# First cross attention of a decoder: queries and keys projected once, the partners of the rotation moved by a shuffle on VectorE

## The chip, the core and the metric

The kernel runs on one core of a Trainium2 chip. The metric is the device time of one launch in microseconds (us). A core has five engines that are named here as the profile names them: PE (TensorE, matrix products; PEld are its weight loads), DVE (VectorE), ACT (ScalarE), POOL (GpSimd) and SP (SyncE, which issues transfers). Each engine works through its own list of instructions in the order of the program, and the engines wait for each other by semaphores.

## What is computed

The reference is a decoder of two layers on 16 sequences of 128 x 256 numbers. The first layer is a causal self-attention with ternary weights, a cross attention with rotary positions, and a mixture of experts; the second has a self-attention, a plain cross attention and a last feed-forward part. A layer norm follows each. The change concerns the first cross attention alone:

```python
q = jnp.einsum('oi,bit->bot', wq, x) + bq[None, :, None]
k = jnp.einsum('oi,bit->bot', wk, c) + bk[None, :, None]
v = jnp.einsum('oi,bit->bot', wv, c) + bv[None, :, None]
...
x_rope, x_pass = (x[..., :d], x[..., d:])
d2 = d // 2
neg_half = jnp.concatenate([-x_rope[..., d2:], x_rope[..., :d2]], axis=-1)
x_rope = x_rope * cos + neg_half * sin
return jnp.concatenate([x_rope, x_pass], axis=-1)
```

There are 16 heads of 8 channels. Of each head, the first four channels are rotated (d = 4): channel 0 is paired with channel 2, and channel 1 with channel 3. In the kernel channels are the 128 partitions, so the partner of a row is the row two below it or two above it.

## The kernel before, in words

The weights are loaded first and the weights of the first attention are made ternary. Then the first self-attention and the first cross attention of all 16 batches are written out as one schedule of beats (`by_beats`, L274). The self-attention (`ternary`, L686) gives two beats to a batch, and the cross attention (`rope_cross_plain`, L906) gives eight, so the beats of the cross attention begin at number 32. A beat holds up to two groups of head scores, then the sums over values, then jobs. Each job has an offset from the first beat of its batch; a job of batch b with offset o is put in beat 32 + 8b + o. Jobs of one beat are issued in the order of their list.

Every instruction of PE, and all those issued through `vec`, `act` and `pool`, keep the order in which they are written (`Written`, L190, and `mm`, L238). So an instruction of an engine that has to wait holds up all that come behind it on that engine.

In a beat of the cross attention (`cross_scores`, L428), PE makes two score tiles named `ps_st`. One has queries in its partitions; DVE takes its row maxima (`nm`). The other has keys in its partitions, is 11 beats behind, and has the maxima added to it by a small product with a 0/1 table (`nmT`, `pick`); ACT takes its exponential into `pT`. Two beats later, PE multiplies these by the values into `ps_o`.

The jobs of a batch in the cross attention are these, with their offsets: `keys` (-10) and `queries` (-5) project and rotate; `values` (5) projects the values; `parts` (8) splits the maxima into three bf16 parts on DVE, and `maxima` (9) transposes them on PE; `out` (20) copies the sums with ACT, `spread` (21) shuffles the denominators on DVE, `invert` (22) takes a logarithm and an exponential of them on ACT, and `divide` (25) multiplies on DVE; `finish` (26) is the output projection with the residual and the statistics of the norm, `scale_rows` (27) applies the norm to the rows of x. For the experts that follow, `gate_turn` (28), and for each pair of batches `gate` (32), `gate_best` (33), `gate_rows` (35) and `places` (39), choose experts and places; four scatters from POOL follow.

Accumulators lie in PSUM. From beat 45 on (`switch`, L265), there are three buffers for score tiles, one for `ps_o`, and one single buffer named `ps_m` for all the products of jobs (L267 and L268): a job's product can only be written once the product before it has been read.

A projection with its rotation (`side`, L920) is now made of two products. One has the weights as they are, and one has the rows of the weights in the order of the partners. Both go into one `ps_m` tile. `rotated` (L800) then adds the bias to the first half and multiplies by the cosines in one DVE instruction, adds the bias to the second half on ACT, multiplies that by the signed sines on POOL, and adds the two on POOL. For queries, POOL then makes four copies of the result (`z`), each with the channels of one head of four left and the others zero.

Another path (`rope_cross_masked`, L984) serves masks that take pairs out. It isn't taken with the inputs here, since the mask has ones alone, but it shares `rotated` and the tables, so it is edited too.

Of the kernel before, what the change touches and what calls it, by code (L numbers as in the profile page):

```python
# [9 lines left out]
F32 = mybir.dt.float32  # L10
# [3 lines left out]
AF = mybir.ActivationFunctionType  # L14
ALU = mybir.AluOpType
# [3 lines left out]
P = 128  # L19
D = 256  # L20
# [11 lines left out]
def kernel(ctx: ExitStack, tc: tile.TileContext, a: dict, out: bass.AP):  # L32
    nc = tc.nc
# [22 lines left out]
    cpool = attn.enter_context(tc.tile_pool(name="ctxpool", bufs=1))  # L56
# [5 lines left out]
    hm = load(const, [P, 26], a["head_masks"], "hm", eng=nc.scalar)  # L62
# [89 lines left out]
    nc.gpsimd.memset(zero, 0.0)  # L152


    xw = load(cpool, [P, 8, P], a["xw"], "xw", eng=nc.gpsimd)
    xb = load(cpool, [P, 6], a["xb"], "xb", eng=nc.gpsimd)
    bv2 = load(cpool, [P, D], a["bv2"].partition_broadcast(P), "bv2", eng=nc.gpsimd)
    rope = load(cpool, [P, 2, D], a["rope"], "rope", eng=nc.gpsimd)
    ctx_t = [load(cpool, [P, D], a["ctx"][b], f"ctx_{b}", eng=nc.gpsimd) for b in range(B)]
# [46 lines left out]
    vec, act, pool = Written(nc.vector), Written(nc.scalar), Written(nc.gpsimd)  # L206
# [31 lines left out]
    def mm(*args, **kw):  # L238

        tc.keep_in_program_order(nc.tensor.matmul(*args, **kw))  # L240
# [391 lines left out]
    ps = pprep.tile([P, 4], F32, name="ps_prep")  # L632
# [9 lines left out]
    for w in range(4):  # L642
        t = pw0.tile([P, 2, D], F32, name="wround", bufs=2)
# [15 lines left out]
    bias = w0.tile([P, 2, D], F32, name="bias")  # L659
# [137 lines left out]
        return 2, 3, causal_scores(pl, kept, qk_scale), jobs, range(B)  # L797


    def rotated(pl, pab, n, dst):  # L800

        t0 = pl[dst].tile([P, D], F32, name=f"rot{n}")
        t1 = pl["w"].tile([P, D], F32, name="rot_t")
        vec.scalar_tensor_tensor(t0, pab[:, 0, :], xb[:, 2 * n : 2 * n + 1], rope[:, 0, :], ALU.add, ALU.mult)
        act.activation(t1, pab[:, 1, :], AF.Identity, bias=xb[:, 2 * n + 1 : 2 * n + 2])
        pool.tensor_tensor(t1, t1, rope[:, 1, :], ALU.mult)
        pool.tensor_tensor(t0, t0, t1, ALU.add)
        return t0
# [88 lines left out]
    def cross_output(pl, b, bias, *products):  # L897

        po = pl["m"].tile([P, D], F32, name="ps_m")
        for n, (w, oT) in enumerate(products):  # L900
            mm(po, lhsT=xw[:, w, :], rhs=oT, start=(n == 0), stop=(n == len(products) - 1))
        xn = pl["w"].tile([P, D], F32, name="xn")
        vec.scalar_tensor_tensor(xn, po, bias, x_t[b], ALU.add, ALU.add)
        return xn, statistics(xn)

    def rope_cross_plain(pl):  # L906

        kept = {}
        bias_of = {}

        def biases(b):

            if b:
                return
            pb = pl["m"].tile([P, 1], F32, name="ps_m")
            mm(pb, lhsT=xw[:, 5, :], rhs=xb[:, 5:6], start=True, stop=True)
            bias_of["ov"] = const.tile([P, 1], F32, name="bias_ov")
            vec.tensor_tensor(bias_of["ov"], pb, xb[:, 4:5], ALU.add)

        def side(b, n, src):  # L920
            pab = pl["m"].tile([P, 2, D], F32, name="ps_m")
            for i in range(2):
                mm(pab[:, i, :], lhsT=xw[:, 2 * n + i, :], rhs=src, start=True, stop=True)
            return rotated(pl, pab, n, "wq"[n])

        def queries(b):
            q = side(b, 0, x_t[b])
            z = pl["q"].tile([P, 4, D], F32, name="z")
            for i in range(4):
                pool.tensor_scalar_mul(z[:, i, :], q, hm[:, 2 + i : 3 + i])  # L930
            kept[b]["qz"] = z

        def keys(b):
            kept[b] = {}
            kept[b]["k"] = side(b, 1, ctx_t[b])

        def values(b):
            pv = pl["m"].tile([P, 2, P], F32, name="ps_m")
            for kc in range(2):
                mm(pv[:, kc, :], lhsT=ctx_t[b][:, kc * P : (kc + 1) * P], rhs=xw[:, 4, :], start=True, stop=True)  # L940
            v = kept[b]["v"] = v8[b % 2]
            for n in range(2):
                act.copy(
                    v[:, :, n::2, 8 * n : 8 * n + 8],
                    pv.rearrange("p c (g i n d) -> p (c g) i n d", g=4, i=2, n=2)[:, :, :, n, :],
                )

        def parts(b):
            maxima_parts(pl, kept[b]["nm"], nmx[b % 2], 4)

        def maxima(b):
            kept[b]["nmT"] = turned_maxima(pl, nmx[b % 2])

        def out(b):
            kept[b] = sums_out(pl, kept[b]["o"])

        def spread(b):
            kept[b] = kept[b], sums_on_values(pl, kept[b])

        def invert(b):  # L960
            inverted(kept[b][1])

        def divide(b):
            ol, l = kept[b]
            vec.tensor_tensor(l, ol, l, ALU.mult)

        def finish(b):
            oT = kept[b][1]
            kept[b] = cross_output(pl, b, bias_of["ov"], (6, oT[:, 0, :]), (7, oT[:, 1, :]))

        def scale_rows(b):
            xn, stats = kept.pop(b)
            scaled(x_t[b], xn, stats)

        jobs = [(8, parts), (9, maxima), (20, out), (21, spread), (22, invert), (25, divide), (-11, biases), (-10, keys),
                (-5, queries), (5, values), (26, finish), (27, scale_rows)]
        for beat, part in ((28, gate_turn), (32, gate), (33, gate_best), (35, gate_rows), (39, places)):
            jobs.append((beat, lambda b, part=part: part(pl, b)))

        for k in range(4):  # L980
            jobs.append((41 + 2 * k, lambda b, k=k: b % 2 and scatter(b - 1 + k // 2, k % 2)))
        return 8, 11, cross_scores(pl, 16, kept, 11), jobs, range(B)

    def rope_cross_masked(st):  # L984

        pl = attention_pools(st)
        v8p = padded(pl["v"], 16, "v8p")
        for b in range(B):
            rot = []
            for n, src in ((0, x_t[b]), (1, ctx_t[b])):  # L990
                pab = pl["m"].tile([P, 2, D], F32, name="ps_m")
                nc.tensor.matmul(pab[:, 0, :], lhsT=xw[:, 2 * n, :], rhs=src, start=True, stop=True)
                nc.tensor.matmul(pab[:, 1, :], lhsT=xw[:, 2 * n + 1, :], rhs=src, start=True, stop=True)
                rot.append(rotated(pl, pab, n, "w"))
            z = pl["w"].tile([P, 4, D], F32, name="z")
            for i in range(4):
                nc.vector.tensor_scalar_mul(z[:, i, :], rot[1], hm[:, 2 + i : 3 + i])
            pv = pl["m"].tile([P, 2, P], F32, name="ps_m")
            for kc in range(2):
                nc.tensor.matmul(  # L1000
                    pv[:, kc, :], lhsT=ctx_t[b][:, kc * P : (kc + 1) * P], rhs=xw[:, 4, :], start=True, stop=True
                )
            vn = pl["w"].tile([P, 2, P], F32, name="v")
            nc.vector.tensor_tensor(vn, pv, bv2.rearrange("p (c d) -> p c d", c=2), ALU.add)
            v = v8p[b % 2]
            nc.vector.tensor_copy(own_channels(v, 16), vn.rearrange("p c (h d) -> p c h d", h=16))
            oT = cross_heads(pl, 16, rot[0], [z[:, i, :] for i in range(4)], v, dict(masked, v=vn))
            xn, stats = cross_output(pl, b, xb[:, 4:5], (5, oT.rearrange("p c q -> p (c q)")))
            scaled(x_t[b], xn, stats)
            for part in (gate_turn, gate, gate_best, gate_rows, places):  # L1010
                part(pl, b)
            for k in range(4 if b % 2 else 0):
                scatter(b - 1 + k // 2, k % 2)

    taken_out = nc.values_load(n_out[0:1, 0:1], min_val=0, max_val=D * D)
    with tc.If(taken_out == 0) as cmp:
        with ExitStack() as st:
            pl, switch = attention_tiles(st, 4)
# [169 lines left out]
    with ExitStack() as st:  # L1188
        pl, switch = attention_tiles(st, 6)
# [422 lines left out]
def layouts(inputs):  # L1612
# [4 lines left out]
    row = np.arange(P)  # L1617
    c = row % 8

    mate = row + np.where(c < 2, 2, np.where(c < 4, -2, 0))  # L1620
    theta = np.float32(1.0) / np.float32(10000.0) ** (np.arange(0, 4, 2, dtype=np.float32) / np.float32(4))
    angle = np.arange(D, dtype=np.float32)[None, :] * theta[c % 2][:, None]
    turn = (c < 4)[:, None]
# [11 lines left out]
    for n in range(2):  # L1635
# [11 lines left out]
        "xw": np.stack([wq.T, wq[mate].T, wk.T, wk[mate].T, wv.T, wo.T] + pairs, 1),  # L1647
        "xb": np.stack([bq, bq[mate], bk, bk[mate], bo, i["L0_xattn_bv"]], 1),
# [44 lines left out]
```

## Time and profile before

| What | Value |
|---|---|
| Median of three runs | 1469.78 us (1468.67 to 1469.87) |
| The profiled execution's own time | 1472.02 us |
| Its span, from first to last instruction | 1470.3 us |
| Mean granted PE clock | 0.959 |
| Beats in which the cross attention runs with the self-attention | up to about 209 us |
| The rest of the first cross attention | 209.62 to some 535 us |
| ACT ACTIVATE pT<-ps_st, 128x1024 | 224 of 1.024 us |
| DVE TENSOR_REDUCE nm<-ps_st, 128x1024 | 1.22 us each |
| PE MATMUL ps_m<-x,xw and ps_m<-ctx,xw | 64 records each, four for a batch |
| DVE SCALAR_TENSOR_TENSOR rot<-ps_m,xb,rope | 32 of 0.483 us |
| ACT ACTIVATE rot_t<-ps_m,xb | 32 of 0.474 us |
| POOL TENSOR_TENSOR rot_t<-rot_t,rope and rot<-rot,rot_t | 32 each, 0.734 and 0.727 us |
| POOL TENSOR_SCALAR z<-rot,hm | 64 of 0.926 us |
| DVE STREAM_SHUFFLE l<-ol, 128x512 | 16 of 0.728 us |

One execution was recorded by the hardware profiler. Times in it are from the start of its span. A timeline row gives the start, the length, the engine, the line, the operation with the tile it writes and those it reads, and the number of instructions merged into the row; in brackets stand the idle time ahead of it and what ended it. Line 199 is a helper's line (`Written`) and so is line 240 (`mm`), so instructions are told apart by the names of their tiles. An f32 product is recorded as two instructions of PE. Granted clock is the share of the full PE clock that the chip allowed.

### The profile page before, as it was taken

Reading aid. Unit: us, or ns where it says so; the run is one execution under the profiler, and the core shown is the slowest. Engines: PE = TensorE matmul, PEld = TensorE weight load, DVE = VectorE, ACT = ScalarE, POOL = GpSimd, SP = SyncE. Lnnn points to the kernel's source line nnn. Section 1 sums busy time; section 2 is a strip of 40 time slices with the busy share of each in tenths; the row PEclk is TensorE's granted clock in tenths of the full one; section 3 lists DMA queues with packets and bytes.
Section 4 is the critical chain, followed back from the end, with each engine's and each line's share of the span. In section 5 each row is a group of like instructions: output and inputs, shape, how many; then the busy total and the mean of one; then the engine's idle time right before and its main releaser. Section 6 shows DMA issues by size and latency. Waiting matters only on the chain. (4 is left out here: it accounts for less than half of the span.)

```text
span 1470.3 us, 28836 instructions
## 1 busy us (share of the span) xinstructions
PE 1338.7 (91%) x11993; PEld 857.1 (58%) x11993; DVE 810.8 (55%) x2085; ACT 595.7 (41%) x1051; POOL 289.6 (20%) x402
## 2 busy tenths in 40 slices
PE   3999999999999938999999589999999989989997
PEld 2656555555555415777888456665555544446666
DVE  6899876777777530100110168876767656543222
ACT  1454426555655611111112135543555556761110
POOL 7000243344444120000000233312121100000000
PEclk9999989999999968999999769999999998999999
DMA  9200000000000006222330411000000000000000
GB/s 300 68 2 2 2 1 2 2 16 16 16 12 12 23 28 193 96 94 92 112 129 15 158 37 31 23 2 1 2 1 2 2 2 1 0 2 15 15 8 22
DMA packets 42780, 57.15 MB, mean 39 GB/s; under 512 B 5929, under 2 KB 32569, under 8 KB 42633
## 3 DMA queue, kind: packets, MB, share of 16 engines
q1 hardware_dynamic: 37192, 41.99, 8.8%
q0 software_dynamic: 4608, 12.34, 2.6%
q8 instruction: 99, 1.62, 0.5%
q10 hardware_dynamic: 832, 0.80, 0.2%
q14 instruction: 49, 0.39, 0.1%
HBM read 38.73 MB, written 16.38 MB: 37 GB/s over the span
## 5 line engine op out<-in xcount | busy, mean ns | idle before, releaser
L199 DVE TENSOR_REDUCE nm<-ps_st 128x4 f32<-128x1024 f32 (+1 forms) x256 | 312.6, 1221 | 123.1 <-PE ps_st L240 119.7
L199 ACT ACTIVATE pT<-ps_st 128x1024 f32<-128x1024 f32 x224 | 229.4, 1024 | 197.3 <-PE ps_st L240 195.5
L199 POOL TENSOR_TENSOR rstd<-ve,nhalf 128x1 f32<-128x1 f32 x112 | 62.7, 561 | 752.1 <-DVE ve L199 630.9
L240 PE MATMUL ps_o<-pT,v 128*32 128x256 f32 (+1 forms) x2560 | 164.5, 347 | 0.5 <-DVE oT L199 0.4
L240 PE MATMUL ps_st<-rot,z 32*128 32x256 f32 x1024 | 147.8, 405 | 2.2 <-DVE nm L199 2.2
L1077 DVE TENSOR_TENSOR ye<-ps_e,b 128x256 f32<-128x256 f32 (+6 forms) x38 | 16.1, 424 | 238.7 <-PE ps_e L1074 238.7
L240 PE MATMUL ps_st<-z,rot 32*128 32x512 f32 x512 | 131.7, 592 | 0.0
L1066 ACT ACTIVATE h<-ps_h,b 128x672 f32<-128x672 f32 (+7 forms) x64 | 46.6, 728 | 204.3 <-PE ps_h L1062 192.3
L1062 PE MATMUL ps_h<-h,w 128*128 128x336 f32 (+7 forms) x512 | 122.1, 399 | 0.0
L1062 PEld LDWEIGHTS ps_h<-h,w 128*128 128x128 f32 x512 | 97.2, 190 | 23.6
L240 PEld LDWEIGHTS ps_o<-pT,v 128*32 128x32 f32 x2560 | 54.6, 108 | 96.2 <-issue 82.4
L240 PE MATMUL ps_st<-nmT,pick 32*128 32x256 bf16 x1024 | 100.7, 274 | 9.8 <-ACT nmT L199 7.4
L240 PEld LDWEIGHTS ps_st<-rot,z 32*128 32x128 f32 x1024 | 91.0, 187 | 14.5 <-issue 5.1
L199 POOL DMA_INDIRECT y<-ys,place x32 | 31.1, 973 | 284.6 <-DVE absT L1195 276.9
L240 PE MATMUL ps_o<-pT,ones 128*32 128x256 f32 x1024 | 79.2, 380 | 0.0
L240 PEld LDWEIGHTS <-pick 32*128 32x128 bf16 x1024 | 30.3, 92 | 79.1 <-issue 72.1
L240 PE MATMUL ps_st<-ctx,z 32*128 32x256 f32 x512 | 73.1, 403 | 0.0
L240 PE MATMUL ps_f<-fxT,fgw 128*128 128x512 f32 x128 | 62.4, 611 | 7.1 <-ACT g L1409 7.1
L1062 PE MATMUL ps_h<-xeT,w 128*128 128x336 f32 (+7 forms) x256 | 65.2, 414 | 4.0 <-DVE xeT L1054 2.1
L1074 PE MATMUL ps_e<-w,h 128*128 128x256 f32 (+6 forms) x304 | 67.3, 379 | 0.0
L240 PE MATMUL ps_st<-z,ctx 32*128 32x512 f32 x256 | 66.6, 596 | 0.0
L1074 PEld LDWEIGHTS ps_e<-w,h 128*128 128x128 f32 (+6 forms) x304 | 54.9, 181 | 11.0 <-issue 1.0
(295 smaller groups left out, 2356.2 us busy)
## 6 DMA issues: line engine op xcount, KB each, us to landing
w<-in_W_dram SPq DMA_DIRECT2D x16, 512.0 KB, 4.0
w<-in_W_dram SPq DMA_DIRECT2D x8, 1024.0 KB, 5.7
xs<-zero SPq DMA_DIRECT2D x42, 128.0 KB, 4.2
xe<-xs SPq DMA_DIRECT2D x32, 128.0 KB, 3.5
ys<-ye SPq DMA_DIRECT2D x32, 128.0 KB, 3.7
x<-in_x_dram SPq DMA_DIRECT2D x16, 128.0 KB, 7.4
ctx<-in_ctx_dram POOLq DMA_DIRECT2D x16, 128.0 KB, 5.9
out_dram<-x SPq DMA_DIRECT2D x16, 128.0 KB, 1.7
```

The lines of the kernel that those rows point to most:

```text
L199: instruction = getattr(self.engine, name)(*args, **kw)
L240: tc.keep_in_program_order(nc.tensor.matmul(*args, **kw))
L1062: nc.tensor.matmul(ps[:, n, 0:H], lhsT=w[:, c, hc * P : (hc + 1) * P], rhs=src[:, c, n * H : (n + 1) * H], start=(c == 0), stop=(c == part ...
L1066: nc.scalar.activation(dst[:, hc, 0:cap].rearrange("p (n t) -> p n t", n=2), ps[:, :, 0:H], AF.Gelu, bias=b12[:, layer, hc : hc + 1],)
L1074: nc.tensor.matmul(ps[0:m], lhsT=h2[:, fc, c : c + m], rhs=w3[:, fc, :], start=(fc == 0), stop=(fc == 3))
L1077: nc.vector.tensor_add(ye[0:m, c // P, :], ps[0:m], b3[0:m])
```

## The change

Each of queries and keys is projected by one product. ACT adds the bias while it copies the product out of PSUM (`biased`). The rows of the partners are made on DVE by a shuffle of that copy within groups of 32 partitions (`mates`), in place of a second product. The cosine product becomes a plain DVE multiplication of two SBUF tiles. The two POOL operations of the rotation and the four that make `z` stay.

The jobs are cut into smaller ones with offsets of their own: `keys` stays at -10 and `turn_keys` comes at -9; `queries` moves from -5 to -6, with `turn_queries` at -5 and `one_head_left` (the four POOL copies) at -4. In the list of jobs, they stand where keys and queries stood, ahead of `values`, `finish` and `scale_rows`.

The tables `xw` and `xb` lose the permuted weights and biases (8 to 6 matrices, 6 to 4 columns), and the indices of the others move down.

```diff
-    xw = load(cpool, [P, 8, P], a["xw"], "xw", eng=nc.gpsimd)
-    xb = load(cpool, [P, 6], a["xb"], "xb", eng=nc.gpsimd)
+    xw = load(cpool, [P, 6, P], a["xw"], "xw", eng=nc.gpsimd)
+    xb = load(cpool, [P, 4], a["xb"], "xb", eng=nc.gpsimd)
...
-    def rotated(pl, pab, n, dst):
-
+
+    mates = [n + (2 if n % 8 < 2 else -2 if n % 8 < 4 else 0) for n in range(32)]
+
+    def biased(pl, ps, n):
+
+        t = pl["w"].tile([P, D], F32, name=f"plain{n}")
+        act.activation(t, ps, AF.Identity, bias=xb[:, n : n + 1])
+        return t
+
+    def rotated(pl, plain, n, dst):
+
+        t1 = pl["w"].tile([P, D], F32, name="rot_t")
+        vec.stream_shuffle(t1, plain, mates)
         t0 = pl[dst].tile([P, D], F32, name=f"rot{n}")
-        t1 = pl["w"].tile([P, D], F32, name="rot_t")
-        vec.scalar_tensor_tensor(t0, pab[:, 0, :], xb[:, 2 * n : 2 * n + 1], rope[:, 0, :], ALU.add, ALU.mult)
-        act.activation(t1, pab[:, 1, :], AF.Identity, bias=xb[:, 2 * n + 1 : 2 * n + 2])
+        vec.tensor_tensor(t0, plain, rope[:, 0, :], ALU.mult)
         pool.tensor_tensor(t1, t1, rope[:, 1, :], ALU.mult)
         pool.tensor_tensor(t0, t0, t1, ALU.add)
         return t0
...
-        def side(b, n, src):
-            pab = pl["m"].tile([P, 2, D], F32, name="ps_m")
-            for i in range(2):
-                mm(pab[:, i, :], lhsT=xw[:, 2 * n + i, :], rhs=src, start=True, stop=True)
-            return rotated(pl, pab, n, "wq"[n])
+        def projected(n, src):
+            pq = pl["m"].tile([P, D], F32, name="ps_m")
+            mm(pq, lhsT=xw[:, n, :], rhs=src, start=True, stop=True)
+            return biased(pl, pq, n)
 
         def queries(b):
-            q = side(b, 0, x_t[b])
+            kept[b]["q"] = projected(0, x_t[b])
+
+        def turn_queries(b):
+            kept[b]["q"] = rotated(pl, kept[b]["q"], 0, "w")
+
+        def one_head_left(b):
             z = pl["q"].tile([P, 4, D], F32, name="z")
             for i in range(4):
-                pool.tensor_scalar_mul(z[:, i, :], q, hm[:, 2 + i : 3 + i])
+                pool.tensor_scalar_mul(z[:, i, :], kept[b]["q"], hm[:, 2 + i : 3 + i])
             kept[b]["qz"] = z
 
         def keys(b):
-            kept[b] = {}
-            kept[b]["k"] = side(b, 1, ctx_t[b])
+            kept[b] = {"k": projected(1, ctx_t[b])}
+
+        def turn_keys(b):
+            kept[b]["k"] = rotated(pl, kept[b]["k"], 1, "q")
...
         jobs = [(8, parts), (9, maxima), (20, out), (21, spread), (22, invert), (25, divide), (-11, biases), (-10, keys),
-                (-5, queries), (5, values), (26, finish), (27, scale_rows)]
+                (-9, turn_keys), (-6, queries), (-5, turn_queries), (-4, one_head_left), (5, values), (26, finish), (27, scale_rows)]
```

`rope_cross_masked` and the host's `layouts` are edited to match.

More of the change, by code (lines that the diff above doesn't have):

```diff
@@ L915, in biases @@
             pb = pl["m"].tile([P, 1], F32, name="ps_m")
-            mm(pb, lhsT=xw[:, 5, :], rhs=xb[:, 5:6], start=True, stop=True)
+            mm(pb, lhsT=xw[:, 3, :], rhs=xb[:, 3:4], start=True, stop=True)
             bias_of["ov"] = const.tile([P, 1], F32, name="bias_ov")
-            vec.tensor_tensor(bias_of["ov"], pb, xb[:, 4:5], ALU.add)
-        def side(b, n, src):
-            pab = pl["m"].tile([P, 2, D], F32, name="ps_m")
-            for i in range(2):
-                mm(pab[:, i, :], lhsT=xw[:, 2 * n + i, :], rhs=src, start=True, stop=True)
-            return rotated(pl, pab, n, "wq"[n])
+            vec.tensor_tensor(bias_of["ov"], pb, xb[:, 2:3], ALU.add)
+        def projected(n, src):
+            pq = pl["m"].tile([P, D], F32, name="ps_m")
+            mm(pq, lhsT=xw[:, n, :], rhs=src, start=True, stop=True)
+            return biased(pl, pq, n)
         def queries(b):
-            q = side(b, 0, x_t[b])
+            kept[b]["q"] = projected(0, x_t[b])
+        def turn_queries(b):
+            kept[b]["q"] = rotated(pl, kept[b]["q"], 0, "w")
+        def one_head_left(b):
             z = pl["q"].tile([P, 4, D], F32, name="z")
             for i in range(4):
-                pool.tensor_scalar_mul(z[:, i, :], q, hm[:, 2 + i : 3 + i])
+                pool.tensor_scalar_mul(z[:, i, :], kept[b]["q"], hm[:, 2 + i : 3 + i])
             kept[b]["qz"] = z
         def keys(b):
-            kept[b] = {}
-            kept[b]["k"] = side(b, 1, ctx_t[b])
+            kept[b] = {"k": projected(1, ctx_t[b])}
+        def turn_keys(b):
+            kept[b]["k"] = rotated(pl, kept[b]["k"], 1, "q")
         def values(b):
@@ L939, in values @@
             for kc in range(2):
-                mm(pv[:, kc, :], lhsT=ctx_t[b][:, kc * P : (kc + 1) * P], rhs=xw[:, 4, :], start=True, stop=True)
+                mm(pv[:, kc, :], lhsT=ctx_t[b][:, kc * P : (kc + 1) * P], rhs=xw[:, 2, :], start=True, stop=True)
             v = kept[b]["v"] = v8[b % 2]
@@ L968, in finish @@
             oT = kept[b][1]
-            kept[b] = cross_output(pl, b, bias_of["ov"], (6, oT[:, 0, :]), (7, oT[:, 1, :]))
+            kept[b] = cross_output(pl, b, bias_of["ov"], (4, oT[:, 0, :]), (5, oT[:, 1, :]))
         def scale_rows(b):
@@ L990, in rope_cross_masked @@
             for n, src in ((0, x_t[b]), (1, ctx_t[b])):
[L991 to L994, printed above, removed]
+                pq = pl["m"].tile([P, D], F32, name="ps_m")
+                nc.tensor.matmul(pq, lhsT=xw[:, n, :], rhs=src, start=True, stop=True)
+                rot.append(rotated(pl, biased(pl, pq, n), n, "w"))
             z = pl["w"].tile([P, 4, D], F32, name="z")
@@ L1000, in rope_cross_masked @@
                 nc.tensor.matmul(
-                    pv[:, kc, :], lhsT=ctx_t[b][:, kc * P : (kc + 1) * P], rhs=xw[:, 4, :], start=True, stop=True
+                    pv[:, kc, :], lhsT=ctx_t[b][:, kc * P : (kc + 1) * P], rhs=xw[:, 2, :], start=True, stop=True
                 )
@@ L1007, in rope_cross_masked @@
             oT = cross_heads(pl, 16, rot[0], [z[:, i, :] for i in range(4)], v, dict(masked, v=vn))
-            xn, stats = cross_output(pl, b, xb[:, 4:5], (5, oT.rearrange("p c q -> p (c q)")))
+            xn, stats = cross_output(pl, b, xb[:, 2:3], (3, oT.rearrange("p c q -> p (c q)")))
             scaled(x_t[b], xn, stats)
@@ L1618, in layouts @@
     c = row % 8
-    mate = row + np.where(c < 2, 2, np.where(c < 4, -2, 0))
     theta = np.float32(1.0) / np.float32(10000.0) ** (np.arange(0, 4, 2, dtype=np.float32) / np.float32(4))
@@ L1646, in layouts @@
         "w0": np.stack([i[f"L0_attn_w_{n}"].T for n in "qkvo"], 1),
-        "xw": np.stack([wq.T, wq[mate].T, wk.T, wk[mate].T, wv.T, wo.T] + pairs, 1),
-        "xb": np.stack([bq, bq[mate], bk, bk[mate], bo, i["L0_xattn_bv"]], 1),
+        "xw": np.stack([wq.T, wk.T, wv.T, wo.T] + pairs, 1),
+        "xb": np.stack([bq, bk, bo, i["L0_xattn_bv"]], 1),
         "bv2": np.concatenate([i["L0_xattn_bv"]] * 2),
```

## The prediction, before the changed kernel was run

> **What bounds the kernel now.** I read the page first, for the share of each engine, then the windows of the first cross attention, then its timelines engine by engine. The chain that ended last reaches back only to 1319.68 us, so it says nothing of this change; the stage does.
>
> ```profile
> PE 1338.7 (91%) x11993; PEld 857.1 (58%) x11993; DVE 810.8 (55%) x2085; ACT 595.7 (41%) x1051; POOL 289.6 (20%) x402
> ```
>
> The columns of the windows are the stretch, its length, then busy time (and instructions) of PE, PEld, DVE, ACT and POOL, granted clock, DMA share, GB/s.
>
> ```profile
> 172.49:209.62 37.13, 33.14 (x324) 20.32 (x324) 31.16 (x71) 11.46 (x22) 9.85 (x14) 0.86 0.00 1
> 209.62:497.79 288.17, 287.73 (x3103) 164.91 (x3103) 219.84 (x441) 169.34 (x264) 117.74 (x143) 1.00 0.03 11
> ```
>
> From 209.62 to 497.79 us, PE is busy 287.73 of 288.17 us, and VectorE and ScalarE have room. That looks like a stage in which each microsecond of matmul taken away is a microsecond won. The timelines say otherwise. PE's timeline shows beats, each opening with the nmT,pick records: scores, then ps_o (the sums), then the beat's jobs.
>
> ```profile
> 303.75 0.28 PE L240 MATMUL ps_st<-nmT,pick 32*128 32x256 bf16 x2
> ...
> 304.93 0.64 PE L240 MATMUL ps_o<-pT,v 128*32 128x256 f32 x8
> 305.50 1.13 PE L240 MATMUL ps_m<-x,xw 128*128 128x256 f32 x4
> 306.56 0.28 PE L240 MATMUL ps_st<-nmT,pick 32*128 32x256 bf16 x2
> ```
>
> This beat's scores take 1.18, its sums 0.57, its job (the two query projections, four records) 1.06: 2.81 us. The next is a pair from the end of the stage, where no batch is left that needs queries:
>
> ```profile
> 486.67 0.28 PE L240 MATMUL ps_st<-nmT,pick 32*128 32x256 bf16 x2
> ...
> 487.85 0.64 PE L240 MATMUL ps_o<-pT,v 128*32 128x256 f32 x8
> 488.42 0.39 PE L240 MATMUL ps_st<-nmT,pick 32*128 32x256 bf16 x4
> ...
> 489.13 1.13 PE L240 MATMUL ps_st<-rot,z 32*128 32x256 f32 x8
> ...
> 490.19 0.64 PE L240 MATMUL ps_o<-pT,v 128*32 128x256 f32 x8
> ```
>
> The beat without a job lasts 1.75, but in the next the second score tile (rot,z) starts only 0.71 after the beat, not 0.02 as above, and scores take 1.77 for 1.18. The reason is on ScalarE: the exponential that frees this score buffer (three, two taken per beat) starts about 1.35 after its beat and takes 1.02, so it ends 2.37 in. A beat shorter than about 2.41 us hands what it lacks to the next. The records hardly show idle time, because the delayed matmuls stop overlapping. So the stage is set by PE and ScalarE in turn.
>
> The page Perfetto Trace Analysis of the Trainium skill (Identifying the Most-Contended Engine) warns that matmul occupancy is not a good measure of distance from the limit. The two readings differ greatly here. By the busy row, 26 projections saved after 209.62, at 1.06/2 = 0.53 each, give 13.8 us. By the beats: with queries, the three beats from 324.67 took 2.81 + 2.12 + 2.59 = 7.52; without them, from 486.67, 1.75 + 2.71 + 2.39 = 6.85. Even a whole query job of 1.06 returns only 0.67. I go by the beats.
>
> **The change, part by part.** I number a beat by its offset modulo 8. Before: keys in 6, queries in 3, finish in 2, gate_turn in 4, values in 5. Only one job per beat uses the single ps_m buffer.
>
> *Queries* move from offset -5 to -6, thus into beat 2, where finish (offset 26) already is; the list puts queries first. From batch 4 on, queries of batch b meet finish of batch b-4: 12 meetings. With one ps_m buffer, PE must hold finish's matmuls until ScalarE has read the projection. Its own price: 0.53 for the projection; the result is readable 0.11 after PE is free (305.50 + 1.06 = 306.56, and VectorE read it at 306.67); the biased copy takes 0.47 (row of rot_t<-ps_m,xb); the handoff back some 0.06, as from an exponential's end to the next score. ScalarE is free then, its exponential ending 2.37 in, the projection at 2.4 or later. So beat 2 grows by 0.53 + 0.64 = 1.17. Behind the waiting finish in PE's order are all later scores.
>
> Beat 3 loses 1.06 and is as 486.67; beat 4 then pays for it, 2.71 for 2.12; beat 5 is 2.39 for 2.59. Sum: +1.17 - 1.06 + 0.59 - 0.20 = **+0.50 per meeting, +6.0**. Queries of batch 3 meet no finish: beats 50 to 53 of this schedule took 2.15 + 2.98 + 1.75 + 2.99 = 9.87; now 2.68 + 1.75 + 2.35 + 2.39 = 9.17, **-0.7**.
>
> *Keys* stay in beat 6 with 0.53 less on PE. But invert is in beat 6 too, and ScalarE is full:
>
> ```profile
> 313.56 1.28 ACT L199 ACTIVATE l<-l 128x512 f32<-128x512 f32 x2
> 314.78 0.47 ACT L199 ACTIVATE rot_t<-ps_m,xb 128x256 f32<-128x256 f32 x1
> 315.39 1.02 ACT L199 ACTIVATE pT<-ps_st 128x1024 f32<-128x1024 f32 x1
> ```
>
> The exponential of beat 7 starts at 315.39, 4.11 after beat 6 began (311.28). With PE 0.53 earlier it would start at 3.58, but invert ends at 3.56 and the biased copy keeps its place behind it. In the last batch, with no keys, that exponential came right behind invert, and the next second score tile 4.63 after beat 6 began (478.50 against 473.87). With the copy it is 4.63 + 0.47 = 5.10, against 5.28 to 5.30 now. Adding what small starts differ, keys win 0.2: I take **-0.23** in eight of the 13 batches left.
>
> In the other five, places runs in beat 7. VectorE gets a shuffle and a multiply for the fused operation it loses: the shuffle of 128x512 takes 0.73, and going from 512 to 256 saves 0.26 in the multiply rows (0.682 to 0.422), so 0.47; multiply 0.42; together 0.89, against 0.48 that ran while it waited anyway. The bounds of the shuffle are 0.36 (half the row) and 0.73 (all of it). Where no places runs, VectorE waits 1.02 before the reduction at 317.73, which covers 0.89. With places, its eight small operations (1.1 us) fill that gap, and the page shows the reduction right behind them. Reduction 7 now ends 0.45 earlier, 0.89 and 1.1 follow, so reduction 0 starts 0.44 later; PE waits for its maxima, as 0.15 at 300.66 already shows. The next beat gives back 0.24 that it spends waiting for ScalarE now: **+0.2 each**. Keys: 8 x -0.23 + 5 x 0.2 = **-0.8**.
>
> *turn_queries* puts 0.89 ahead of scale_rows in beat 3. The rows of x are then ready 3.95 after that beat began, and gate_turn wants them at 4.10: hidden by 0.15; with the dear shuffle it costs 0.1 in 12 batches. *POOL* keeps its six operations per batch, z one beat later; z takes 3.64 us and has four beats, so this costs nothing; if it ran past them, the first scores of the batch would wait. Its scatters stand between the same groups. *DMA*: xw and xb shrink by a quarter and a third in the first loads, long before keys at 128; nothing.
>
> *Before 209.62* three batches' keys and queries run among the first attention. If VectorE sets the pace, six turns cost 6 x 0.41 = +2.5; if PE does, -3.2. PE waited 1.81 and 0.40 for reductions at 193 to 197, so I lean to VectorE, less what the removed operation gives back: **+0.5**.
>
> Sum: 6.0 - 0.7 - 0.8 + 0.5 = **+5.0**. The profiled execution took 1472.0 (span 1470.3 and 1.7 around it), so it goes to 1477.0. It lay 2.2 above the median of 1469.78, so the median goes to 1474.7.
>
> **The clock.** PE's clock was halved from 196.91 to 207.15, around that wait of 1.81. The page TensorE: Matmul & The Clock Gate of the Trainium skill (Part 1) says the gate closes after an idle window of some 3.4 us. Here waits of 0.40 and 1.81 within 5 us were enough, while 0.80 at 209.62 changed nothing. By the rule and by the row alike my 0.64 per 20 us is safe; but by the row, the altered waits at 193 to 200 can drop this half-speed stretch or add one, up to 5 us (half of 10.24) either way. The rule would leave this out; I keep it in the range.
>
> **Rivals.** Measurement can tell about 0.2% (2.9 us) from no change.
> - *PE sets the pace throughout*: every saved projection pays, 13.8 after 209.62 and 3.2 before: 1469.8 - 17.0 = 1452.8. For it speaks the busy row; against it the end of the stage, 0.67 for 1.06. It decides if beats below 2.41 us hand nothing on. Faster, 6%.
> - *finish doesn't wait* (its bank is not the projection's): beat 2 grows by 0.53 only, so -0.14 per meeting, -1.7 in place of +6.0: -2.7, 1467.1. Against it: ps_m has one buffer after the switch. 12%, a third of it faster.
> - *The half-speed stretch goes*: 1470, 10%, no change.
> - *Dear shuffle, or one more half-speed stretch*: shuffle 0.26 more in five keys and some 0.1 in 12 queries, +2.5, 1477; with the clock 1480. 22%, slower.
> - *The sum as worked out*, within 2.5: 50%, of which 5 within 0.2%.
>
> So slower 67%, within 0.2% 23%, faster 10%. The range, 1467 to 1481, reaches from the finish that doesn't wait to a further half-speed stretch, and leaves PE's full gain out.
>
> **What would show it.** Right: in the beats of 58 and every eighth after it, PE idle 0.6 us or more before ps_m<-l,xw, released by the biased copy on ScalarE; the next beat at 1.75 and gate_turn's beat near 2.7; after keys' beats of about 2.3, the exponential of beat 7 right behind the biased copy; in batches with places, the maxima about 0.4 later. The shuffle's row should read 0.4 to 0.5. Wrong: no idle time before ps_m<-l,xw, or beats of 1.75 followed by scores of 1.18, or PE waiting for x before gate_turn.

## The result and the profile after

The changed kernel took 1478.55 us (median of four runs, 1477.64 to 1479.86) against 1469.70 for the kernel before (four runs, 1468.67 to 1469.87). The ratio is 1.0063, with a 95% interval of 1.0049 to 1.0076: slower by 0.6%. The forecast was 1474.7, in a range of 1467 to 1481, with slower as the likeliest side. The profiled execution took 1477.77 (forecast 1477.0), with a span of 1476.1 and a mean granted clock of 0.958.

First the page's row of the engines, then the windows of the same two stretches as before.

```profile
PE 1333.3 (90%) x11929; PEld 847.0 (57%) x11929; DVE 822.8 (56%) x2149; ACT 595.4 (40%) x1051; POOL 293.5 (20%) x402
```

```profile
172.49:209.62 37.13, 31.73 (x298) 18.80 (x288) 31.67 (x75) 11.18 (x22) 11.90 (x16) 0.80 0.00 1
209.62:497.79 288.17, 273.73 (x2928) 151.20 (x2930) 222.95 (x478) 161.68 (x253) 119.43 (x141) 0.99 0.03 11
```

PE's weight loads fell from 11993 to 11929: the 64 records of the second product are gone. But in 209.62 to 497.79 PE is now busy 273.73 of 288.17 us, where it was 287.73. These are the same times and not quite the same beats. The beats that filled this stretch before now lie from 208.97 to 508.24, and there PE is busy 284.83 of 299.27 us. Either way, some 14 us are idle where 0.4 were. Two waits of 209 to 510 us make up this time (total us, number, longest):

```profile
PE ps_m L243 <- DVE nmx L199: 7.7, 5, 1.6
PE ps_m L240 <- ACT plain L199: 6.8, 12, 0.6
```

The second row was forecast; it is the meeting of queries and finish on the single `ps_m`. The first had 0.2 in all before, once. It was forecast to grow by about 0.4 a time, and it now takes 1.5 in the mean.

**The meeting**, in PE's timeline of a batch without `places`:

```profile
326.29 0.64 PE L240 MATMUL ps_o<-pT,v 128*32 128x256 f32 x8
326.86 0.70 PE L240 MATMUL ps_m<-x,xw 128*128 128x256 f32 x2
328.13 1.13 PE L240 MATMUL ps_m<-l,xw 128*128 128x256 f32 x4 [0.56 <-ACT plain L199]
329.19 0.28 PE L240 MATMUL ps_st<-nmT,pick 32*128 32x256 bf16 x2
...
330.94 0.39 PE L240 MATMUL ps_st<-nmT,pick 32*128 32x256 bf16 x4
```

The output projection (`ps_m<-l,xw`) follows the projection of the queries, and stands 0.56 us until ScalarE has copied it. All later scores stand with it. The next beat, 329.19 to 330.94, is 1.75 long, as forecast.

**The keys**, in ScalarE's timeline of the same batch; beat 6 began at 314.84:

```profile
317.12 1.28 ACT L199 ACTIVATE l<-l 128x512 f32<-128x512 f32 x2
318.31 0.46 ACT L199 ACTIVATE plain<-ps_m,xb 128x256 f32<-128x256 f32 x1
318.66 1.01 ACT L199 ACTIVATE pT<-ps_st 128x1024 f32<-128x1024 f32 x1
```

The exponential of beat 7 begins at 318.66, right behind the biased copy and 3.82 after its beat 6 began; before it was 4.11.

**The places**, in VectorE's timeline of a batch that has them, first before, then after:

```profile
297.22 0.19 DVE L199 TENSOR_TENSOR own_at<-oh,at 128x32 f32<-128x32 f32 x1
297.44 0.19 DVE L199 TENSOR_REDUCE place_f<-own_at 128x4 f32<-128x32 f32 x1
297.54 0.16 DVE L199 TENSOR_SCALAR past<-gf 128x4 f32<-128x4 f32 x1
```

```profile
298.58 0.44 DVE L199 STREAM_SHUFFLE rot_t<-plain 128x256 f32<-128x256 f32 x1
298.92 0.42 DVE L199 TENSOR_TENSOR rot<-plain,rope 128x256 f32<-128x256 f32 x1
299.25 0.17 DVE L199 TENSOR_TENSOR at<-ps_m,free 128x16 f32<-128x16 f32 x1
...
299.45 0.52 DVE L199 TENSOR_TENSOR own_at<-oh,at 128x32 f32<-128x32 f32 x1
300.00 0.19 DVE L199 TENSOR_REDUCE place_f<-own_at 128x4 f32<-128x32 f32 x1
300.10 0.65 DVE L199 TENSOR_SCALAR past<-gf 128x4 f32<-128x4 f32 x1
...
301.26 1.22 DVE L199 TENSOR_REDUCE nm<-ps_st 128x4 f32<-128x1024 f32 x1
```

GpSimd's timeline of after has the two operations of the same keys' rotation, at the same time:

```profile
299.11 0.81 POOL L199 TENSOR_TENSOR rot_t<-rot_t,rope 128x256 f32<-128x256 f32 x1 [3.83 <-DVE rot_t L199]
300.00 0.73 POOL L199 TENSOR_TENSOR rot<-rot,rot_t 128x256 f32<-128x256 f32 x1
```

The `at` of before began at 297.02 (from the trace), right behind the reduction. After, the shuffle and the multiplication come ahead of it, and more: `own_at` (0.19 before) ends at 299.97, just after the first of them (299.92), and `past` (0.16 before) at 300.75, just after the second (300.73). Before, the second ended at 297.26 (from the trace), and `own_at` began at 297.22: the two hardly touched. The shuffle and the multiplication of queries and keys cost what was forecast (the mean of 32 in ns, behind the total):

```profile
L199 DVE STREAM_SHUFFLE rot_t<-plain 128x256 f32<-128x256 f32 x32 | 13.9, 435 | 0.0
L199 DVE TENSOR_TENSOR rot<-plain,rope 128x256 f32<-128x256 f32 x32 | 13.2, 414 | 0.0
```

Beats measured from one `nmT,pick` to the next, as medians over the batches, with beats numbered as in the prediction (a sum can differ from its row by a few hundredths through rounding):

| Beat | 6 | 7 | 0 | 1 | 2 | 3 | 4 | 5 | sum |
|---|---|---|---|---|---|---|---|---|---|
| no places, before | 2.81 | 1.75 | 3.34 | 1.97 | 3.53 | 2.81 | 2.12 | 2.59 | 20.93 |
| no places, after | 2.38 | 1.75 | 3.47 | 1.97 | 4.78 | 1.75 | 2.73 | 2.40 | 21.23 |
| places, before | 2.81 | 1.94 | 2.16 | 2.22 | 2.94 | 2.81 | 2.12 | 2.59 | 19.61 |
| places, after | 2.38 | 1.94 | 2.30 | 3.56 | 4.08 | 1.75 | 2.71 | 2.39 | 21.11 |

### The profile page after: what moved, and what is told of

The parts are those of the page before. It is cut to its first block, busy times and chain, and to the rows that moved or that the text cites. A ratio compares the mean times of both kernels' runs of the same rounds, so it can differ in the third digit from the quotient of the medians.

```text
span 1476.1 us, 28745 instructions
## 1 busy us (share of the span) xinstructions
PE 1333.3 (90%) x11929; PEld 847.0 (57%) x11929; DVE 822.8 (56%) x2149; ACT 595.4 (40%) x1051; POOL 293.5 (20%) x402
```

## The experiments

Each ran in five rounds with the kernel before on the same chip; ratios are to that. In these rounds the kernel before took 1466.20 to 1477.95 us in 58 runs, with medians of 1470.04 to 1472.36, so the ratios are to be compared and not the times. "The stage" means the shift of the last beats of the cross attention in the profiled execution against the profiled execution of before; for the changed kernel it is +10.45 us. Theory at the outset: the loss is the meeting on `ps_m` and, in batches with places, VectorE waiting for GpSimd. Rivals: ScalarE is simply full, so the place of the queries doesn't matter; and the shuffle's own time delays the maxima.

**1. Queries in beats of their own** (the changed kernel, their three jobs one beat later):

```diff
-                (-9, turn_keys), (-6, queries), (-5, turn_queries), (-4, one_head_left), (5, values), ...
+                (-9, turn_keys), (-5, queries), (-4, turn_queries), (-3, one_head_left), (5, values), ...
```

> The changed kernel with queries back in the beat that has no other product (offset -5), turn_queries at -4 and one_head_left at -3; all else as changed. Theory A (finish waits behind queries for the single ps_m buffer): PE no longer waits before ps_m<-l,xw; per meeting the beat of finish shrinks by 1.1 to 1.2, the next three go from 1.75 + 2.71 + 2.39 = 6.85 to about 2.28 + 2.2 + 2.5 = 7.0, so 1.0 to 1.1 less in each of 12 batches: 1466 us, or 1463 if the second half-speed stretch of PE goes too. Theory B (the loss is VectorE's added work and what it does behind POOL, wherever queries stand): within 2 us of 1478.5.

Measured: 1467.47 against 1470.59, ratio 0.9981 (0.9967 to 0.9995). The sum of the eight beats falls from 21.23 to 20.19 in batches without places. PE's wait for the copy is gone; its timeline has the output projection directly behind the sums, and the queries a beat later:

```profile
320.00 0.64 PE L240 MATMUL ps_o<-pT,v 128*32 128x256 f32 x8
320.57 1.13 PE L240 MATMUL ps_m<-l,xw 128*128 128x256 f32 x4
...
322.81 0.64 PE L240 MATMUL ps_o<-pT,v 128*32 128x256 f32 x8
323.38 0.70 PE L240 MATMUL ps_m<-x,xw 128*128 128x256 f32 x2
```

So the meeting cost 1.04 per batch: 0.6 more than before the change, and 0.44 that the saved product gives when queries stand alone. The stage is now 4.19 ahead of before: the change with this one offset altered is no longer slower, and its interval is just clear of no change (0.2% faster). The other row, `nmx`, kept its 7.7 us.

**2. The keys' whole rotation five beats later:**

```diff
-                (-9, turn_keys), (-6, queries), (-5, turn_queries), ...
+                (-4, turn_keys), (-6, queries), (-5, turn_queries), ...
```

> The changed kernel with turn_keys moved from offset -9 to -4, out of the beat of places; queries stay where the change put them. Theory A with the trace of the changed kernel: in the five batches with places, PE no longer waits 1.3 to 1.6 for the maxima, and keys keep what they win: 1.3 less in each of five, 1472 us. Theory B' (that wait has nothing to do with the place of turn_keys): 1478.5. If theory B of VectorE's total load were right, moving the same work within a batch would change nothing: 1478.5 as well.

Measured: 1472.41 against 1470.59, ratio 1.0009 (0.9997 to 1.0021). Beat 1 of batches with places falls from 3.56 to 2.07, the eight beats from 21.11 to 19.90; PE no longer waits for `nmx`, and `own_at` and `past` have 0.19 and 0.16 again. The meeting stays. This takes both the shuffle and the collision with GpSimd away, so it doesn't separate them; the next one does.

**3. Only GpSimd's two operations of the keys later**, the shuffle and the multiplication left at -9:

```diff
         pool.tensor_tensor(t1, t1, rope[:, 1, :], ALU.mult)
         pool.tensor_tensor(t0, t0, t1, ALU.add)
...
-                (-9, turn_keys), (-6, queries), (-5, turn_queries), (-4, one_head_left), (5, values), ...
+                (-9, turn_keys), (-6, queries), (-5, turn_queries), (-4, sum_keys), (-4, one_head_left), (5, values), ...
```

(The two operations shown keep their text and become a function of their own, which `sum_keys` calls for keys; `rot_t` has buffers of its own for each kind.)

> The changed kernel with only the two POOL operations of turn_keys moved to offset -4; the shuffle and the multiplication on VectorE stay at -9, ahead of places. Theory C (contention: two small operations of places take 0.52 and 0.65 instead of 0.19 and 0.16 since POOL works at that moment): they are back at 0.19 and 0.16, and the wait for the maxima falls by 0.82 in five batches: 4 us less, 1474.4. Theory D (the wait is the shuffle's and multiplication's own 0.85 of VectorE, as in the prediction's sum): 1478.5, unchanged.

Measured: 1476.07 against 1470.59, ratio 1.0038 (1.0023 to 1.0053). The shuffle is where it was, and the small operations have their old lengths:

```profile
298.59 0.44 DVE L199 STREAM_SHUFFLE rot_t<-plain 128x256 f32<-128x256 f32 x1
...
299.45 0.19 DVE L199 TENSOR_TENSOR own_at<-oh,at 128x32 f32<-128x32 f32 x1
...
299.78 0.16 DVE L199 TENSOR_SCALAR past<-gf 128x4 f32<-128x4 f32 x1
300.45 1.22 DVE L199 TENSOR_REDUCE nm<-ps_st 128x4 f32<-128x1024 f32 x1
```

The reduction begins at 300.45 and not at 301.26, 0.81 earlier from the same start. Beat 1 falls from 3.56 to 2.77, and PE's wait for `nmx` from 7.7 to 3.7. So 0.8 of the loss per batch with places is the collision. What is left of the wait is the own time of the shuffle and the multiplication: the second experiment, which takes them away too, brings beat 1 down by 0.7 more. In the whole stage this edit gave 3.3 back (+7.13 against +10.45), less than 5 x 0.8, since beat 2 grew by 0.2 in three of the other batches, which wasn't followed up. The intervals of the ratios touch (1.0063 had 1.0049 to 1.0076), so it is the trace that shows the cause.

**4. Both moved**: queries as in the first, the keys' rotation two beats later in batches that meet places, that is every second one.

```diff
-                (-9, turn_keys), (-6, queries), (-5, turn_queries), (-4, one_head_left), (5, values), ...
+                (lambda i: -7 if i % 2 else -9, turn_keys), (-5, queries), (-4, turn_queries), (-3, one_head_left), (5, values), ...
```

> Queries as in the first of these runs (-5, -4, -3), and turn_keys at -7 for odd batches, whose beat is that of places, and at -9 for even ones. Theory A: the two gains add up, 12 x 1.05 and 5 x about 1, so 1478.5 - 17.6 = about 1461, below the kernel before (1469.8) by 0.6%: the saved projections then pay about half of what PE has less to do. A rival: with no wait for ps_m, VectorE is the next bound in odd batches and the second gain is lost: 1466, as with queries alone.

Measured: 1458.13 (1455.39 to 1461.51) against 1470.59, ratio 0.9917 (0.9899 to 0.9934). This beats both kernels. The eight beats take 20.19 and 18.88; the stage is 10.40 ahead of before. The two gains add up: against the changed kernel, the stage won 14.6 in the first experiment and 7.0 in the second, and 20.9 here. Here GpSimd's rotation (the first of its rows: 298.78 to 299.59) runs beside a reduction of maxima from PSUM instead, and that reduction has its usual 1.22:

```profile
298.92 1.22 DVE L199 TENSOR_REDUCE nm<-ps_st 128x4 f32<-128x1024 f32 x1
```

**5. The keys' biased copy on VectorE**, from the kernel with both moved:

```diff
-        act.activation(t, ps, AF.Identity, bias=xb[:, n : n + 1])
+        if n == 1 and ordered[0]:
+            vec.tensor_scalar(t, ps, xb[:, n : n + 1], None, ALU.add)
+        else:
+            act.activation(t, ps, AF.Identity, bias=xb[:, n : n + 1])
```

> The kernel with both jobs moved (e4), and the biased copy of keys made by VectorE instead of ScalarE. Theory A' (in the beat of keys ScalarE is full with the exponential and invert, so the copy pushes the exponential of beat 7 back and eats most of what keys save): that exponential starts right behind invert, 0.33 earlier; 0.3 less in the seven or eight batches without places, where nothing else is late, 2.5 us below e4; up to 4 if the others win too. Rival (the copy is not in the way; VectorE's work decides now): no gain, or a loss of up to 2 us, since VectorE gets 0.48 more in 16 batches.

Measured: 1458.57 against 1470.04, ratio 0.9925 (0.9901 to 0.9948): nothing to be told from the one before it. The beats did become shorter, 20.05 and 18.75, by 0.13 to 0.14 each, some 1.7 us in the stage. In the profiled execution the beats before 232 us came out 2.5 later, with a half-speed stretch of PE of 20.5 us where the kernel before it had 13.7. The ninth asks whether the edit causes that.

**6. The move alone**: the kernel before, with two products per projection, its job of the queries at -6.

```diff
-                (-5, queries), (5, values), (26, finish), (27, scale_rows)]
+                (-6, queries), (5, values), (26, finish), (27, scale_rows)]
```

> The kernel before, with queries at offset -6 instead of -5 and nothing else changed: two products for each projection, no shuffle. Theory A (the meeting with finish costs, whatever is projected): finish waits for VectorE's and ScalarE's reads, one after the other: the beat of finish grows by 1.06 + 0.11 + 0.48 + 0.10 + 0.47 + 0.06 = 2.28, the next three change by -1.06 + 0.59 - 0.20, so +1.6 in 12 batches: 1489. Theory B (place is free, the shuffle costs): 1470, as before.

Measured: 1506.03 against 1470.04, ratio 1.0242 (1.0215 to 1.0268). The direction is that of the meeting, at twice the size. Beats 2 to 5 of batches without places take 5.79 + 1.75 + 3.88 + 2.40 = 13.82 against 11.05 before. PE's timeline shows two waits in place of one:

```profile
341.10 1.13 PE L240 MATMUL ps_m<-x,xw 128*128 128x256 f32 x4
343.37 1.13 PE L240 MATMUL ps_m<-l,xw 128*128 128x256 f32 x4 [1.14 <-ACT rot_t L199]
...
349.71 0.44 PE L243 MATMUL ps_m<-ident,x 128*128 128x128 f32 x2 [1.14 <-DVE x L199]
```

The second is gate_turn waiting for the normed rows; these wait for `rstd`, which GpSimd calculates, and GpSimd's timeline has it behind the queries' six operations:

```profile
343.41 0.72 POOL L199 TENSOR_TENSOR rot_t<-rot_t,rope 128x256 f32<-128x256 f32 x1 [7.89 <-ACT rot_t L199]
...
345.04 3.63 POOL L199 TENSOR_SCALAR z<-rot,hm 128x256 f32<-128x256 f32 x4
348.64 0.57 POOL L199 TENSOR_TENSOR rstd<-ve,nhalf 128x1 f32<-128x1 f32 x1
```

**7. The first four batches' queries in their own beats**, the others as in the changed kernel:

```diff
-                (-9, turn_keys), (-6, queries), (-5, turn_queries), (-4, one_head_left), (5, values), ...
+                (-9, turn_keys),
+                (lambda i: -5 if i < 4 else -6, queries), (lambda i: -4 if i < 4 else -5, turn_queries),
+                (lambda i: -3 if i < 4 else -4, one_head_left), (5, values), ...
```

> The changed kernel with queries, turn_queries and one_head_left at -5, -4, -3 for batches 0 to 3 alone, which meet no finish; from batch 4 on as changed. If the second half-speed stretch near 205 us comes from where the early queries stand: the stretch is shorter, as in e1 (13.7 instead of 20.5 us), the stage is 2.4 us shorter at beat 50, and the rest is as changed: 1476. If the stretch doesn't hang on that: 1478.5, with half speed for 20 us as before.

Measured: 1476.77 against 1470.04, ratio 1.0051 (1.0032 to 1.0070). Its half-speed stretch is 13.7 us in the trace, the changed kernel's 20.5, and the stage ends 2.6 earlier (+7.82). But the interval overlaps that of the changed kernel, so by the times alone it isn't told apart. Nor does the place of these queries alone decide the stretch: the fifth and the ninth have them here too, and 20.5 us.

**8. The move with GpSimd's part cut off**: the sixth, with the two operations of the rotation at -5 and `z` at -4.

```diff
-                (-5, queries), (5, values), (26, finish), (27, scale_rows)]
+                (-6, queries), (-5, sum_queries), (-4, one_head_left), (5, values), (26, finish), (27, scale_rows)]
```

> This is the kernel before, with both products of the queries moved to offset -6, as in the experiment that moved the whole job, but with GpSimd's part cut off: its two operations of the rotation at -5 and its four copies (z) at -4. Moving the whole job cost 36 us where 19 were expected. Theory A: the meeting on ps_m costs 1.6 per batch (1.06 more product, a wait of 1.14, less what the next beats give back), and the other 1.2 came from GpSimd, where rstd of finish stood behind the queries' six operations, so that x came late and gate_turn waited 1.14. Then with the parts cut, beat 4 falls from 3.88 to about 2.7, the wait for x goes, and the time is 1489 (1486 to 1492). Theory B: x is late because finish itself starts late, whatever GpSimd does: beat 4 stays at 3.9, and the time stays at 1506.

Measured: 1484.68 against 1472.36, ratio 1.0098 (1.0073 to 1.0122). `rstd` comes first on GpSimd, and gate_turn follows the sums at once; the meeting itself stays:

```profile
330.64 1.13 PE L240 MATMUL ps_m<-l,xw 128*128 128x256 f32 x4 [1.14 <-ACT rot_t L199]
...
335.20 0.64 PE L240 MATMUL ps_o<-pT,v 128*32 128x256 f32 x8
335.77 0.44 PE L243 MATMUL ps_m<-ident,x 128*128 128x128 f32 x2
```

```profile
333.25 0.57 POOL L199 TENSOR_TENSOR rstd<-ve,nhalf 128x1 f32<-128x1 f32 x1 [10.47 <-DVE ve L199]
333.80 0.71 POOL L199 TENSOR_TENSOR rot_t<-rot_t,rope 128x256 f32<-128x256 f32 x1
```

Beat 4 falls from 3.88 to 2.69, and beats 2 to 5 take 5.79 + 1.75 + 2.69 + 2.39 = 12.62, 1.57 more than before; 12 of these are the 17 of the stage, with 1.6 won earlier. So theory A holds here: of the extra 2.8 per batch in the sixth, 1.6 is the meeting and 1.2 GpSimd's queue. The time was 1.3 below the range expected, and more so against its own rounds: 12.3 over the kernel before, where some 19 were expected. The stage lost 17.0, and the second layer begins only 13.5 later. Uncut, the move cost 36 us, and cut 12. No run has the change under study with its job of the queries uncut, but this suggests what cutting it saved there.

**9. VectorE's copy only from batch 4 on** (the fifth, with `b > 3` choosing VectorE):

```diff
-            kept[b] = {"k": projected(1, ctx_t[b])}
+            kept[b] = {"k": projected(1, ctx_t[b], b > 3)}
```

> The kernel with both groups of jobs moved and the keys' biased copy on VectorE, but for batches 0 to 3 the copy stays on ScalarE, as those keys run among the first attention. With the copy on VectorE for all batches, the beats of batches 4 to 15 became shorter by 0.13 each, but the first beats came out 2.5 later, with a half-speed stretch of 20.5 in place of 13.7. Theory A: VectorE is the tighter engine there, and its four added copies bring the longer stretch; then the stretch is 13.7 again, the beats after stay at 20.05 and 18.75, and the time is 1456.5 (1454.5 to 1458). Theory B: the stretch is drawn by other things; it stays at 20.5 and the time at 1458.5.

Measured: 1459.42 against 1472.36, ratio 0.9916 (0.9893 to 0.9940). The beats after stay as in the fifth (20.06 and 18.77), but the half-speed stretch is 20.5 here too, against theory A, in the one execution profiled. The ratio has room for both theories. This profiled execution was also 3.7 later than the fifth's from 40 us on, in a part that is the same in both kernels. Two rows of PE there, of the fifth and then of this one, show the same 16 products at full and at half speed:

```profile
36.13 1.16 PE L240 MATMUL ps_st<-qk 32*128 32x128 f32 x16
```

```profile
37.53 2.08 PE L240 MATMUL ps_st<-qk 32*128 32x128 f32 x16
```

So a few us of a profiled execution before 232 us can come from the clock alone, and I take none of the early differences as an effect of an edit.

## Why the prediction was right, and where its sizes were off

The side and the mechanism were right, and the total lay 3.9 under the median, inside the range. Term by term, in us at the end of the stage; a measured value says how much later, against before, its stretches of beats ended than they began, summed over the batches:

| Term | Forecast | Measured |
|---|---|---|
| 12 meetings of queries and finish (beats 2 to 5) | 12 x 0.50 = 6.0 | +6.1 (0.37 to 0.62 each) |
| Keys, eight batches without places (beats 6 to 1) | 8 x -0.23 = -1.8 | 7 x -0.30 = -2.1, the eighth below |
| Keys, five batches with places (beats 6 to 1) | 5 x 0.2 = +1.0 | +5.4 (1.01 to 1.27 each) |
| Queries of batch 3 | -0.7 | -0.6 |
| Before 209.62 | +0.5 | +1.7 at beat 50, with the keys of batch 3 |
| After the last meeting | 0 | -0.1 |
| Sum | +5.0 | +10.4 (the stage: +10.45) |

- **The meeting**: in the medians without places, beat 2 grew by 1.25 (forecast 1.17), beat 3 lost 1.06, beat 4 paid 0.61 (0.59), beat 5 won 0.19 (0.20). PE's wait for the copy was 0.56 where 0.64 was worked out; the rival in which finish doesn't wait is refuted by that row and by experiment 1.
- **The beat rule** (a beat under 2.41 hands its shortage on) held: beats of 1.75 were followed by 2.73. The rival in which PE sets the pace would have given a faster kernel; instead, the stage grew, with 14 us more in which PE is not busy.
- **Places**: the mis-sized term. The prediction had the shuffle and multiply (0.89) ahead of eight small operations of 1.1 us, as in the trace before. Reduction 7 did end 0.43 earlier, counted from beat 6. But the small operations took 0.81 longer, since GpSimd's rotation now ran beside them. Against this, the shuffle and the multiply delayed what follows by 0.67 only, not 0.89, since consecutive operations overlap in the trace: 298.58 to 299.25. Together the reduction starts 0.67 + 0.81 - 0.43 = 1.05 later than before, where 0.44 was forecast, and 0.11 comes back in beat 2 (1.14 more there, against 1.25), where 0.24 was counted on: 0.94 and not 0.2. (In the table, what comes back stands in the row of the meetings.) The step that failed is "its eight small operations (1.1 us)": their length was carried over from a place where GpSimd's rotation hardly touched the two that grew. With it failed the term for POOL, put at nothing because its load stayed the same: where its operations run did change. Experiment 3 shows it: with GpSimd's two operations elsewhere, 0.79 of the beat is back.
- **Which operations suffer**: the page GPSIMD Engine Reference of the Trainium skill (1. Specifications) says that GpSimd shares its SBUF interfaces with VectorE, with contention for VectorE's instructions that have two SBUF inputs or run in a two-port mode. The rows fit: `own_at` has two SBUF inputs and went from 0.19 to 0.52; the reduction `place_f`, with one, stood beside the second GpSimd operation and kept its 0.19; maxima from PSUM kept 1.22. `past` has one SBUF input and went from 0.16 to 0.65; that it runs in such a mode fits, but no run here shows it. The order of starting counts too: the multiplication of the rotation has two SBUF inputs and starts 0.19 ahead of GpSimd's `rot_t`; it kept its 0.41, and `rot_t` took 0.81 for 0.73. I had priced only VectorE's added work and left this rule out.
- **The trace of before had shown the collision**, at another place. In all five batches in which GpSimd's `rot_t` ran beside it, VectorE's `both` took 0.75; in the last batch, with nothing beside it, 0.17:

```profile
328.72 0.74 POOL L199 TENSOR_TENSOR rot_t<-rot_t,rope 128x256 f32<-128x256 f32 x1 [1.93 <-DVE oh L199]
328.73 0.75 DVE L199 TENSOR_TENSOR both<-oh 128x16 bf16<-128x16 f32 x1
```

- **turn_queries** was hidden by VectorE's slack, but with less to spare than forecast. GpSimd's rotation now runs beside the scaling of x as well, which took 0.82 in all 12 meetings, where it takes 0.40 alone. In the batch shown above, whose beat 3 began at 329.19, the rows of x were ready after 4.05 us (forecast 3.95) and gate_turn began after 4.11; beat 4 takes 2.73 (forecast 2.71):

```profile
332.27 0.82 POOL L199 TENSOR_TENSOR rot_t<-rot_t,rope 128x256 f32<-128x256 f32 x1 [0.97 <-DVE rot_t L199]
332.42 0.82 DVE L199 TENSOR_SCALAR x<-xn,mv,rstd 128x256 f32<-128x256 f32 x1
```

- **Before 209.62**: the beat that began there came 0.65 earlier than before. Half speed then lasted until 215.18, 20.5 us in all (10.24 before), and the loss of 1.7 stands at beat 50. The prediction kept up to 5 us for the clock in its range and not in the sum. In the nine kernels that followed, PE was at half speed for 6.8 to 20.5 us there, and experiment 9 speaks against the cause I had thought of, so what decides its length is open.

The span grew by 5.8 only, not by 10.45. In the profiled execution of before, two of the last scatters waited longer than the usual 1.71 for the one ahead, with the experts behind them:

```profile
540.47 0.96 POOL L199 DMA_INDIRECT xs<-x,place  x1 [3.16 <-DMA xs<-x,place]
545.00 0.96 POOL L199 DMA_INDIRECT xs<-x,place  x1 [3.57 <-DMA xs<-x,place]
```

After has one such wait, 2.63: 2.4 less in all. A half-speed dip of 3.4 us at 1320, which the trace of before has, is missing after; the products behind it, 7.4 later than before ahead of the dip, are 5.75 later behind it, so 1.7 less. Some 0.6 went in between. So 10.45 - 2.4 - 0.6 - 1.7 = 5.75. None of this was in the prediction: it was luck that the profiled execution came so near to the forecast 1477.0, by two misses of opposite sign. The medians differ by 8.85, nearer to the stage.

## What to carry to other kernels

Where one PSUM buffer serves all the products of a schedule, two projections in one beat cost more than their length: give each job a beat, also after it has been halved. An operation moved on one engine takes its collisions with it: look at what runs on GpSimd beside the small VectorE operations on the critical path, and don't carry their lengths over from a place without that. The trace at hand can show the price: look for one operation that has two lengths, here 0.75 and 0.17. When an operation is moved past others, count the queues of every engine that it issues to; here cutting GpSimd's part off was worth 1.2 us per batch, and other offsets alone lie between the change as made and the fourth experiment (ratios to before of 1.0063, 1.0049 to 1.0076, and 0.9917, 0.9899 to 0.9934).

## What was not expected of the hardware

- VectorE's operations of 0.16 to 0.19 us took 0.52 to 0.75 beside a GpSimd operation of 0.73 to 0.81, each ending 0.02 to 0.05 after it: they seem to wait for its end rather than to share. The scaling of x, with more work (128x256), ended 0.15 after it, which fits as well.
- The stretches at half clock in this kernel come in lengths of 3.4, 6.8, 10.2, 13.7, 20.5, 37.5, 41.0 and 44.4 us, which are multiples of some 3.41. The same beats had 10.24 after waits of 0.40 and 1.81 us (before), and 20.5 after 0.77 and 1.41 (after).
- At the start, full speed came between 33.1 and 34.4 us in nine of the profiled executions, and at 42.4 and 43.2 in experiments 6 and 9, whose first score beats came 3.5 later than before and 3.7 later than in experiment 5, in the same code.
